# A four-layer graph network on one core: no check between the two steps of layer 3, and one sum and one branch at the end

## The chip, the cores and the metric

The kernel runs on one core of a Trainium2 chip. The metric is the device time of one execution in microseconds (us), as the median of several. A core has five instruction engines that run side by side and wait for one another through semaphores: TensorE (PE, with its weight loads as PEld), VectorE (DVE), ScalarE (ACT), GpSimd (POOL) and SyncE (SP), which here issues most DMAs.

## The reference

A node matrix x of 3327 x 256 goes through four layers, each as x + layer(relu(layernorm(x))), with one adjacency matrix adj of 3327 x 3327 (about 1% of it is not zero, every value is at least 0). Everything is float32.

```python
# layer 0: adj @ (h @ W.T + b)
# layer 1: sim = tanh(adj * adj), of each row the 700 largest entries, times a projected h
vals, idx = jax.lax.top_k(filt, 700)
# layer 2: relu(D^-1/2 (adj + I) D^-1/2 @ (h @ W.T))
# layer 3: two steps
R = S + I;  R = R / R.sum(-1, keepdims=True)            # S is adj
for n in range(2):
    probs = softmax((Xa @ W1.T @ W2.T) @ (Xa @ W3.T).T)
    A = probs, of each row the largest entries until their sum reaches 0.9, renormalised
    Xf = R @ Xf
    Xa = A @ Xa
    Z = Z + Xf @ U1[n].T + Xa @ U2[n].T
out = x + layernorm(X + Z)
```

Two things in it depend on the data. Layer 1 keeps 700 entries of a row, which is all of them unless a row has more than 700 that are not zero. Layer 3 needs, for every row of 3327 probabilities, the threshold at which the kept ones reach 0.9.

## The kernel before

**Tiles.** The 3327 nodes are padded to T = 26 tiles of 128 rows. The products with the adjacency matrix (layers 0 to 2, and `Xf = R @ Xf` in layer 3) take tiles in pairs, m and m + 13, and form the four blocks of a pair from seven products, as Strassen and Winograd do. In layer 3 these are `PropagatedPair` (matmuls L1182), whose operands are "slabs" of 832 KB in three buffers, loaded by SyncE (L1147) and partly corrected by POOL (L1151).

**Attention in layer 3.** For each of the two steps and each tile: eight logits matmuls in four chunks of two PSUM banks (L962), each chunk evicted by ScalarE with exp and a row sum (L983, `exp_of_logits`); then `search_steps`, which looks for the row's threshold. That is a chain of six small ScalarE operations (L1000 to L1005), a ScalarE pass over the 3328 columns (`junk_a`, relu, L1016), a second pass (sign, L1021; for the first tile of a step, which is `alone`, VectorE does it, L1019), and VectorE passes: L1032, four partial passes L1041 with 26 `max` of eight (L1045), some small operations, and L1061, which zeroes what is below the threshold in the tile `e` and sums the rest. TensorE then turns `e` in 128 x 128 blocks (`pt`, L186), ScalarE copies them (`eT`, L189), and TensorE multiplies them with the nodes (L197). The tiles of the second step come in the order 0, 13, 1, 14, and so on; three are in work at a time.

**Guards.** The search starts from an estimate and can fail for a row. `failed(step, st)` compares the kept sums of all 26 tiles with their targets, lets a matmul with ones (`pf`, L1093) add up the rows that failed, and reduces that by threes (L1099) to four levels of counts, of which the last holds the total. `if_failed` then loads the total into a register of every engine (L1406) and branches (`tc.If`, L1407); behind the branch lies a nested tree that leads to each tile, with code that searches it again (`by_least`, and `general` behind a further branch) and recomputes what came from it. The kernel holds one such check between the steps and one after the second step. A third guard, for layer 1: `most1` is the largest count of entries in a row, copied as an integer into `flag`; at the end `at_end()` loads it (L1732), and `tc.If(loaded[0] > TOPK)` (L1735) leads to a second pass over layers 1 to 3, `all_layers(True)`, in which layer 1 searches for the 700th entry. In the data at hand no count is above zero and no row above 700, so each branch passes its code over.

**What sets the order.** On TensorE the order is written out by hand (`tc.manual_schedule(engines=PE_ALONE)`, with `spread`, `merged` and `plan` naming which steps go between which matmuls). A planner places the instructions of the other engines by costs and priorities; `tc.high_priority()` and `tc.issue_after(x)` bend it. Each engine runs its instructions in the planned order. A branch parts the program: nothing is planned across it. So the check between the steps separates the end of step one (the propagation of pair 12, phase one, and the logits of tiles 0 and, in part, 13 of step two) from the rest. Two lines stand behind it: the `memset` of one column of `w`, and `only_exp_and_ln()` (L873), a load of ScalarE's function table.

Of the kernel before, what the change touches and what calls it, by code (L numbers as in the profile page):

```python
# [11 lines left out]
F32 = mybir.dt.float32  # L12
I32 = mybir.dt.int32
# [4 lines left out]
ALU = mybir.AluOpType  # L18
# [6 lines left out]
P = 128  # L25
T = 26
NP = T * P
# [5 lines left out]
TOPK = 700  # L33
# [13 lines left out]
def kernel(  # L47
# [22 lines left out]
    nc = tc.nc  # L70


    const = ctx.enter_context(tc.tile_pool(name="const", bufs=1))
# [798 lines left out]
    def only_exp_and_ln():  # L872
        tc.keep_in_program_order(nc.scalar.preload_act_table_set("natural_log_exp_and_others"))  # L873

    def layer_3(again, h3, kT0, ksum0, left, at_end):
        tag = "b" if again else "a"

        only_exp_and_ln()
        with ExitStack() as lctx:
            big, ep, w3, sm3 = (  # L880
                lctx.enter_context(tc.tile_pool(name=f"{n}{tag}", bufs=b))
                for n, b in (("big", 1), ("ep", 3), ("w3", 2), ("sm3", 4))
            )
            layer_3_in(tag, big, ep, w3, sm3, h3, kT0, ksum0, left, at_end)

    def layer_3_in(tag, big, ep, w3, sm3, h3, kT0, ksum0, left, at_end):

# [9 lines left out]
        w = big.tile([P, 7 * P], F32, name="w")  # L899
# [174 lines left out]
        LEVELS = 3  # L1074
# [262 lines left out]
        spare = []  # L1337
# [64 lines left out]
        def if_failed(step, flags, st, kT, then, scratch, at_last):  # L1402
            def inside(level, i, gen):
                if i * 3**level >= T:
                    return
                n = nc.values_load(flags[level].bitcast(I32)[0:1, i : i + 1])  # L1406
                with tc.If(n > 0):  # L1407
                    if level:
                        with tc.tile_pool(name=f"gen{step}", bufs=1) if not gen else nullcontext(gen) as g:
                            for k in range(3):  # L1410
                                inside(level - 1, 3 * i + k, g)
                        if level == LEVELS:
                            at_last()
                    else:
                        e, den, bad = by_least(step, i, kT, gen, st, scratch)
                        then(i, e, den, f"t{i}")
                        n_bad = nc.values_load(bad)
                        with tc.If(n_bad > 0):
                            then(i, *general(step, i, kT, gen, scratch), f"g{i}")

            inside(LEVELS, 0, None)

        kT1, ksum1 = new_keys(f"1{tag}", big)
# [11 lines left out]
        with tc.manual_schedule(engines=PE_ALONE):  # L1435

            st0, made, dens, props = new_state("0"), {}, {}, []
# [85 lines left out]
            for i in range(EARLY):  # L1523
                plan = {}
# [21 lines left out]
            for m in range(T):  # L1546
                interleaved = m + AHEAD < T and m not in APART
                plan, later = passes_apart(0, finder) if interleaved else (passes(finder), {})
                plan = merged(plan, left_over)
# [63 lines left out]
        def redo_second_steps_first():  # L1613
            run(exp_of_logits(1, 0, kT1, first_e, first_parts, "again"))

        if_failed(0, flags0, st0, kT0, redo_first, lambda name: first_e, redo_second_steps_first)

        nc.vector.memset(w[:, 0:1], 0.0)  # L1620
        only_exp_and_ln()
        with tc.manual_schedule(engines=PE_ALONE):
            st1 = new_state("1")
            run(find(1, 0, st1))
            rows_of_first(H - 2)
            p = props.pop(0)
            propagate_first(T - 2, merged(spread(steps_of_second, 0, 6), {3: [lambda: p.scale(last_exp)], 8: [p.turn], 12: [p.sums]}))
            p = props.pop(0)
            second = find(1, ORDER[1], st1)

            def pass_of_second():
                with tc.issue_after(last_exp[-1].ins):
                    next(second)

            plan = {0: [lambda: p.scale(last_exp)], 3: [p.turn], 8: [p.sums], 15: [lambda: next(second), pass_of_second], 19: [pass_of_second]}
            propagate_first(T - 1, merged(spread(prepare(1, ORDER[2], kT1), 4, 10), plan))
            run(second)
            finder = find(1, ORDER[2], st1)
            fs.append(new_nodes(f"fs{tag}")[:, :, :D])
            for k in range(0, T, H):  # L1640
                for a, b in ((k, k + 6), (k + 6, k + H - 1)):
                    nc.scalar.dma_start(fs[0][:, a:b, :], fs_dram[:, a:b, :])
            rows_of_first(H - 1)

            def propagate_second(m, at):
                acc = new_acc(f"f1_{m}")
                run(propagated_steps(acc, 1, m, fs[0]), at)
                return acc

            rows = Rows(1, vs)  # L1650
            rows.begin(0)
            flags1 = []
            ts = new_ts(1)
            ys, stores = {}, []
            for i, m in enumerate(ORDER):
                ahead = ORDER[i + AHEAD] if i + AHEAD < T else None
                plan, later = passes_apart(1, finder) if ahead else (passes(finder), {})
                if i == 0:
                    p, q = props
                    plan = merged(plan, {2: [p.scale, q.scale], 4: [p.turn], 5: [p.sums, q.turn], 6: [q.sums]})  # L1660
                acc = rows.finish(m, plan)
                if i == 0:
                    nc.sync.dma_start(gs, ln_g.partition_broadcast(P))
                    nc.sync.dma_start(bs, ln_b.partition_broadcast(P))
                ys[m] = attention_of_second_step(m, acc, dens.pop(m), f"{m}")
                plan = spread(prepare(1, ahead, kT1)) if ahead else {}
                if i + 1 < T:
                    plan = merged(plan, {20: [lambda: rows.begin(ORDER[i + 1])]}, later)
                else:
                    plan = {4: [lambda: flags1.extend(failed("1", st1))]}  # L1670
                if i == 1:
                    with tc.issue_after(last_found[-1].ins):
                        for c in CUTS:
                            combine(fs[0], ts, *c)
                p, phase = m % H, m // H
                if p == 0:

                    finish3(m, ys.pop(m), propagate_second(m, plan)[:, :D], f"{m}")()
                else:
                    if not phase:  # L1680
                        pair = PropagatedPair(1, p, fs[0], ts)

                        def stores_of_last():

                            with tc.issue_after(pair.loaded.ins):
                                while stores:
                                    stores.pop(0)()

                        plan = merged(plan, {22: [stores_of_last]})
                    units = H * len(PHASES[phase])  # L1690
                    run(pair.steps(phase), {k * units // T: v for k, v in plan.items()})
                    if not phase:
                        pair.half()
                    else:
                        both = pair.whole()
                        for j, k in ((1, m), (0, p)):
                            if pair.last and not j:
                                pair.ended()
                            stores.append(finish3(k, ys.pop(k), both[:, j, :], f"{k}"))
                finder = find(1, ahead, st1) if ahead else None  # L1700
            for store in stores:
                store()

        def redo_second(m, e, den, name):
            y = attention_of_second_step(m, rows_times(e, vs, w3, f"a1_{name}"), den, name)
            finish3(m, y, propagate_second(m, {})[:, :D], name)()

        at_end()
        spare.append(ep.tile([P, NP], F32, tag="e", name=f"spare{tag}"))
        if_failed(  # L1710
            1, flags1, st1, kT1, redo_second, lambda name: ep.tile([P, NP], F32, tag="e", name=name), lambda: None
        )


    def all_layers(again, at_end):
        with tc.manual_schedule(engines=PE_ALONE):
            lctx, h3, kT0, ksum0, left = layers_0_to_2(again)
            lctx.close()
            if not again:

                nc.vector.tensor_reduce(most, counts, AX.X, ALU.max)
                pm = one_bank("pm")
                nc.tensor.transpose(pm[:1, :P], most, ident)
                nc.vector.tensor_reduce(most1, pm[:1, :P], AX.X, ALU.max)
                nc.vector.tensor_copy(flag, most1)
        layer_3(again, h3, kT0, ksum0, left, at_end)

    most = const.tile([P, 1], F32, name="most")
    most1 = const.tile([1, 1], F32, name="most1")
    flag = const.tile([1, 1], I32, name="flag")  # L1730
    loaded = []
    all_layers(False, lambda: loaded.append(nc.values_load(flag[0:1, 0:1])))  # L1732


    with tc.If(loaded[0] > TOPK):  # L1735
        all_layers(True, lambda: None)


# [44 lines left out]
```

## The time and the profile before

| | us |
|---|---|
| three runs | 2583.54, 2582.86, 2580.24 (median 2582.86) |
| the profiled execution: its time | 2582.32 |
| its span, first to last instruction | 2580.5 |
| layers 0 to 2, until about | 960 |
| layer 3, first step, until the check | 960 to 1796.5 |
| around the check: TensorE busy | 8.7 of 15.0 (1796.5 to 1811.5) |
| second step: TensorE busy | 748.9 of 757.5 (1811.5 to 2569) |
| from the last arithmetic to the end of the span | 11.5 |

TensorE's mean granted clock over the span is 0.994 of full speed. One execution is profiled; its time is the metric, and its span is 1.8 us shorter, because the time also holds what lies ahead of the first and behind the last recorded instruction. Engines' busy times are given as sums over the span. In a timeline, brackets hold how long the engine had been idle before the instruction and which instruction is inferred to have ended that; a "q" behind an engine's name stands for the engine's queue of register, branch and semaphore instructions, which do not count as busy.

### The profile page before, as it was taken

To read this page: it belongs to the slowest core of one execution; us is meant where nothing else is said; L and a number is where in the kernel's file an instruction comes from. 1 tells how busy PE (TensorE), PEld (TensorE's weight loads), DVE (VectorE), ACT (ScalarE), POOL (GpSimd) and SP (SyncE) were. 2 spreads that over 40 slices of the span, in tenths; PEclk is the share of its full clock that TensorE was granted. 3 is DMA by queue.
4 is the path that set the end of the run, shared out by engine and by line. 5 is a ranking of instruction groups with operands and counts; after the bars stand their busy time and mean duration, and the time that the engine had idled before them with its cause. 6 is when DMAs were issued, how large, how long until landed. Compare 5 with 4: busy or idle time off the path is not lost. (4 is left out here: it accounts for less than half of the span.)

```text
span 2580.5 us, 47702 instructions
## 1 busy us (share of the span) xinstructions
PE 2514.0 (97%) x17929; PEld 2255.6 (87%) x17929; DVE 2082.3 (81%) x5538; ACT 1083.7 (42%) x2055; POOL 293.1 (11%) x485
## 2 busy tenths in 40 slices
PE   7999999999999999999999999998999999999997
PEld 7999999999999998878787878787888888888886
DVE  6667788888878778787778787784899899899994
ACT  3110123343111115555656566653555555555551
POOL 2000010000000001000000000000021122212132
PEclk9999999999999999999999999999999999999999
DMA  6677765555788865323232323232433343344342
GB/s 222 191 227 249 220 197 182 166 173 171 250 294 269 280 208 186 107 65 107 69 103 92 107 67 102 61 113 97 159 119 106 112 135 111 112 141 130 106 135 84
DMA packets 181794, 388.47 MB, mean 151 GB/s; under 512 B 19742, under 2 KB 78747, under 8 KB 181531
## 3 DMA queue, kind: packets, MB, share of 16 engines
q1 hardware_dynamic: 153210, 364.31, 43.7%
q10 hardware_dynamic: 28320, 20.80, 2.5%
q8 instruction: 147, 2.41, 0.4%
q14 instruction: 117, 0.95, 0.1%
HBM read 315.44 MB, written 67.89 MB: 149 GB/s over the span
## 5 line engine op out<-in xcount | busy, mean ns | idle before, releaser
L189 ACT COPY eT_a<-pt_a 128x512 f32<-128x512 f32 (+1 forms) x364 | 195.8, 554 | 361.2 <-PE pt_a L186 361.0
L197 PE MATMUL a<-h3a,eT_a 128*128 128x256 f32 x1352 | 325.7, 383 | 0.2 <-ACT eT_a L189 0.2
L197 PE MATMUL a<-vs,eT_a 128*128 128x256 f32 x1352 | 320.3, 381 | 0.2 <-ACT eT_a L189 0.2
L1045 DVE MAX8 cand_a<-w 128x8 f32<-128x128 f32 x1352 | 290.0, 279 | 4.5
L197 PEld LDWEIGHTS a<-h3a,eT_a 128*128 128x128 f32 x1352 | 245.7, 191 | 37.5 <-issue 5.7
L197 PEld LDWEIGHTS a<-vs,eT_a 128*128 128x128 f32 x1352 | 244.7, 190 | 30.2 <-ACT eT_a L189 0.7
L557 PE MATMUL acc_a<-tsa,s_a 128*128 128x128 f32 (+1 forms) x2028 | 269.1, 275 | 0.0
L557 PE MATMUL acc_a<-rhs,a_a 128*128 128x128 f32 (+1 forms) x2028 | 251.4, 277 | 0.1
L557 PE MATMUL acc_a<-tsa,a_a 128*128 128x128 f32 x2028 | 250.3, 275 | 0.9 <-DVE tsa L351 0.9
L557 PEld LDWEIGHTS acc_a<-tsa,s_a 128*128 128x128 f32 x2028 | 248.2, 192 | 0.3
L557 PEld LDWEIGHTS acc_a<-rhs,a_a 128*128 128x128 f32 x2028 | 239.3, 192 | 2.2 <-ACT rhs L436 0.4
L557 PEld LDWEIGHTS acc_a<-tsa,a_a 128*128 128x128 f32 x2028 | 239.1, 192 | 2.1 <-DVE tsa L351 1.3
L1041 DVE SCALAR_TENSOR_TENSOR w<-e_a,t_a 128x896 f32<-128x896 f32 x208 | 225.0, 1082 | 4.4
L983 ACT ACTIVATE e_a<-pl_a 128x1024 f32<-128x1024 f32 x208 | 177.8, 860 | 108.6 <-PE pl_a L962 108.6
L186 PE MATMUL pt_a<-ident,e_a 128*128 128x128 f32 x1352 | 199.9, 274 | 6.9 <-DVE e_a L1061 6.6
L186 PEld LDWEIGHTS pt_a<-ident,e_a 128*128 128x128 f32 x1352 | 165.9, 141 | 36.5 <-DVE e_a L1061 7.2
L1151 POOL TENSOR_TENSOR slab3a<-slab3a,ident 128x128 f32<-128x128 f32 x100 | 104.2, 1043 | 814.5 <-DMA slab3a<-in_adj_t_dram 379.1
L1061 DVE SCALAR_TENSOR_TENSOR e_a<-e_a,all_least 128x3328 f32<-128x3328 f32 x52 | 194.4, 3739 | 1.8
L1032 DVE SCALAR_TENSOR_TENSOR w<-e_a,t_a 128x3328 uint8<-128x3328 f32 x52 | 191.7, 3686 | 4.0
L395 ACT ACTIVATE xT_a<-pt_a 128x512 f32<-128x512 f32 x52 | 30.8, 593 | 356.6 <-PE pt_a L391 300.5
L1182 PEld LDWEIGHTS f0a<-tsa,slab3a 128*128 128x128 f32 x1352 | 160.2, 192 | 16.9 <-issue 13.9
L688 ACT ACTIVATE a_a<-a_a 128x640 f32<-128x640 f32 (+1 forms) x156 | 101.4, 665 | 174.2 <-DVE a_a L687 152.9
(246 smaller groups left out, 4224.2 us busy)
## 6 DMA issues: line engine op xcount, KB each, us to landing
slab3a<-s_dram SPq DMA_DIRECT2D x100, 832.0 KB, 4.6
a_a<-in_adj_t_dram SPq DMA_DIRECT2D x312, 256.0 KB, 4.1
slab3a<-in_adj_t_dram SPq DMA_DIRECT2D x79, 832.0 KB, 4.6
a_a<-in_adj_t_dram SPq DMA_DIRECT2D x156, 320.0 KB, 3.8
s_dram<-s_a SPq DMA_DIRECT2D x78, 256.0 KB, 4.9
s_dram<-s_a SPq DMA_DIRECT2D x39, 320.0 KB, 5.2
x_dram<-x_a ACTq DMA_DIRECT2D x39, 256.0 KB, 3.5
s_dram<-a_a SPq DMA_DIRECT2D x26, 256.0 KB, 5.2
```

The source lines that it names most:

```text
L186: nc.tensor.transpose(pt[:, j, :], e[:, k * P : (k + 1) * P], ident)
L189: last_turned.append(nc.scalar.copy(eT[:, : len(blocks), :], pt[:, : len(blocks), :]))
L197: nc.tensor.matmul(acc[:, :width], ready[g][:, j, :], rhs[:, k, :], start=(k == 0), stop=(k == T - 1))
L557: nc.tensor.matmul(self.acc[:, g, at : at + wide], quads[n][:, k - CUTS[c][0], :], t, start=(k == 0 and n in (1, 4)), stop=(k == H - 1 and ...
L688: nc.scalar.activation(a, a, AF.Tanh)
L983: last_exp.append(nc.scalar.activation(dst, src, AF.Exp, accum_out=parts[:, c : c + 1]))
L1032: nc.vector.scalar_tensor_tensor(junk, e, t, e, ALU.is_lt, ALU.mult, accum_out=got)
L1041: nc.vector.scalar_tensor_tensor(w[:, : (b - a) * P], eg, t, eg, ALU.is_lt, ALU.mult, accum_out=below[:, g : g + 1])
L1045: nc.vector.max(cand[:, 8 * k : 8 * k + 8], w[:, (k - a) * P : (k - a + 1) * P])
L1061: nc.vector.scalar_tensor_tensor(e, e, least, e, ALU.is_ge, ALU.mult, accum_out=st["kept"][:, m : m + 1])
L1151: nc.gpsimd.tensor_tensor(x[:, p, :], x[:, p, :], ident, ALU.add)
L1182: nc.tensor.matmul(self.accs[bank][:, c * P : (c + 1) * P], a, self.right(n, k), start=start, stop=last.get(bank) == (n, k), skip_group_ch ...
```

## The change

The check after step one, the check after step two, the `memset` and the table load behind the first are now in the program only in the second pass (`if again`). In the first pass the last tile's step `last_flags` forms one number, `redo`: 1 if `most1` is over 700, plus the total of failures of the first step, plus that of the second. After the store of the results one register is loaded from it, and one branch leads to the second pass, which holds the checks of single tiles and the search of layer 1. The integer copy `flag` is gone. A failed tile, which was redone alone before, would now cost a whole second pass.

```diff
-        if_failed(0, flags0, st0, kT0, redo_first, lambda name: first_e, redo_second_steps_first)
-
-
-
-        nc.vector.memset(w[:, 0:1], 0.0)
-        only_exp_and_ln()
+        if again:
+            if_failed(0, flags0, st0, kT0, redo_first, lambda name: first_e, redo_second_steps_first)
+            nc.vector.memset(w[:, 0:1], 0.0)
+            only_exp_and_ln()
+
         with tc.manual_schedule(engines=PE_ALONE):
             st1 = new_state("1")
...
-                    plan = {4: [lambda: flags1.extend(failed("1", st1))]}
+                    def last_flags():
+                        flags1.extend(failed("1", st1))
+                        if not again:
+                            nc.vector.scalar_tensor_tensor(
+                                redo, most1, float(TOPK), flags0[LEVELS], ALU.is_gt, ALU.add
+                            )
+                            nc.vector.tensor_tensor(redo, redo, flags1[LEVELS], ALU.add)
+
+                    plan = {4: [last_flags]}
...
-        at_end()
-        spare.append(ep.tile([P, NP], F32, tag="e", name=f"spare{tag}"))
-        if_failed(
-            1, flags1, st1, kT1, redo_second, lambda name: ep.tile([P, NP], F32, tag="e", name=name), lambda: None
-        )
-
-
-    def all_layers(again, at_end):
+        if again:
+            spare.append(ep.tile([P, NP], F32, tag="e", name=f"spare{tag}"))
+            if_failed(
+                1, flags1, st1, kT1, redo_second, lambda name: ep.tile([P, NP], F32, tag="e", name=name), lambda: None
+            )
+
+
+    def all_layers(again):
...
-                nc.vector.tensor_copy(flag, most1)
-        layer_3(again, h3, kT0, ksum0, left, at_end)
+        layer_3(again, h3, kT0, ksum0, left)
...
-    flag = const.tile([1, 1], I32, name="flag")
-    loaded = []
-    all_layers(False, lambda: loaded.append(nc.values_load(flag[0:1, 0:1])))
-
-
-    with tc.If(loaded[0] > TOPK):
-        all_layers(True, lambda: None)
+    redo = const.tile([1, 1], F32, name="redo")
+    all_layers(False)
+    n_redo = nc.values_load(redo.bitcast(I32)[0:1, 0:1])
+
+
+    with tc.If(n_redo > 0):
+        all_layers(True)
```

More of the change, by code (lines that the diff above doesn't have):

```diff
@@ L873, in only_exp_and_ln, with layer_3 @@
         tc.keep_in_program_order(nc.scalar.preload_act_table_set("natural_log_exp_and_others"))
-    def layer_3(again, h3, kT0, ksum0, left, at_end):
+    def layer_3(again, h3, kT0, ksum0, left):
         tag = "b" if again else "a"
@@ L883, in layer_3, with layer_3_in @@
             )
-            layer_3_in(tag, big, ep, w3, sm3, h3, kT0, ksum0, left, at_end)
-    def layer_3_in(tag, big, ep, w3, sm3, h3, kT0, ksum0, left, at_end):
+            layer_3_in(again, tag, big, ep, w3, sm3, h3, kT0, ksum0, left)
+    def layer_3_in(again, tag, big, ep, w3, sm3, h3, kT0, ksum0, left):
         def new_ts(step):
```

## The prediction

> **What bounds the kernel now.** I read the page's busy shares first, then the table of stretches around the check between the two steps of layer 3, the timelines of TensorE and ScalarE there, the instructions of the check's own lines, and last the end of the run. The page's first section:
>
> ```profile
> PE 2514.0 (97%) x17929; PEld 2255.6 (87%) x17929; DVE 2082.3 (81%) x5538; ACT 1083.7 (42%) x2055; POOL 293.1 (11%) x485
> ```
>
> TensorE is the bound. After the check it hardly stops again (the waits of PE from 1796 us on hold, beside the check, only 2.5, 1.1, 0.3 and 0.2 us), so what it loses at the check arrives at the end unless another engine takes it. The timeline of TensorE there (start, length, what, and in brackets the idle time before it and who ended that):
>
> ```profile
> 1795.86 0.71 PE L1182 MATMUL f0a<-h3a,slab3a 128*128 128x128 f32 x4
> 1799.73 0.46 PE L1182 MATMUL f0a<-h3a,slab3a 128*128 128x128 f32 x2 [3.15 <-ACT mean_a L1001]
> 1803.31 4.14 PE L962 MATMUL pl_a<-kT_1a,qT 64*128 64x512 f32 x8 [3.12 <-DVEq L1407]
> 1807.38 2.94 PE L1182 MATMUL f0a<-h3a,slab3a 128*128 128x128 f32 x24
> 1810.26 1.35 PE L962 MATMUL pl_a<-kT_1a,qT 64*128 64x512 f32 x8
> ```
>
> Two holes, 3.15 and 3.12 us: the first is TensorE's own branch, the second its wait for VectorE's (ACT in the first bracket is inferred; ScalarE was done). The logits at 1803.31 then take 4.14 us, where the eight that began at 1790.68 took 1.99. The table of stretches says why: the column after POOL is the granted clock.
>
> ```profile
> 1800.20:1803.30 3.10, 0.00 (x0) 0.02 (x1) 0.00 (x0) 0.60 (x3) 0.00 (x0) 0.52 0.09 30
> 1803.30:1807.40 4.10, 4.09 (x9) 2.25 (x9) 4.01 (x6) 3.88 (x3) 0.56 (x2) 0.53 0.25 73
> 1807.40:1811.60 4.20, 4.20 (x34) 3.49 (x33) 3.94 (x7) 1.85 (x6) 0.00 (x0) 1.00 0.16 24
> ```
>
> The lines of the branches (duration in ns min/median/max, first and last start):
>
> ```profile
> L1407 PEldq COMPARE_BRANCH  x2: 3342/3620/3897, 1795.3 to 2562.9; - x2
> L1407 DVEq COMPARE_BRANCH  x2: 72/72/72, 1798.8 to 2569.0; - x2
> L1407 DVEq EVENT_SEMAPHORE  x4: 21/21/21, 1803.1 to 2572.7; - x4
> L1732 SPq TENSOR_LOAD <-flag x1: 273/273/273, 2573.5 to 2573.5; - x1
> L1735 SPq EVENT_SEMAPHORE  x9: 17/17/17, 2576.8 to 2579.1; - x9
> ```
>
> VectorE's branch at 1798.8 takes 0.07 us by its record, but its next instruction stands at 1803.1. So a branch over skipped code costs an engine 3 to 5 us, on TensorE inside the branch's record, on the others as silence after it. At the end the last arithmetic (DVE L1293) stops at 2569.1 us and the span at 2580.5: 11.4 us of stores landing, two branches in turn (L1407, L1735) and a closing barrier.
>
> [...]
>
> **The change part by part.** The instruction order of the changed program, engine by engine, is that of the old one without the check, but for the moves named here.
>
> *The check between the steps goes.* On the old clock: TensorE is done at 1796.57, and without the branch issues its next two matmuls at once (0.25 us), then the eight logits of tile 13, chunks 0 and 1 (1.99 at full clock), then 24 propagation matmuls (2.94). That is 1801.8; chunk 2 ends at 1802.8. Chunk 3 needs the PSUM bank of chunk 1, and here ScalarE decides:
>
> ```profile
> 1797.03 0.20 ACT L983 ACTIVATION_READ_ACCUMULATOR e_a<-pl_a 128x1 f32 x1
> 1799.11 0.21 ACT L1000 ACTIVATE parts_a<-parts_a 128x5 f32<-128x5 f32 x1 [1.88 <-ACTq L1407]
> 1803.52 3.07 ACT L1016 ACTIVATE junk_a<-e_a,t_a 128x3328 uint8<-128x3328 f32 x1 [2.66 <-POOLq L1407]
> 1806.59 1.00 ACT L983 ACTIVATE e_a<-pl_a 128x1024 f32<-128x1024 f32 x1
> ```
>
> Without its 1.88 us it goes from 1797.2 through the small chain L1000 to L1005 (1.75 us, from 1799.11 to 1800.86) to 1799.0. In the new order the eviction of chunk 0 stands before the pass L1016, not behind it: 1.0, to 1800.0. Then the pass, 3.07, to 1803.1; then the eviction of chunk 1 with its accumulator, 1.2, to 1804.3. So TensorE waits 1.5 us at chunk 3 and is through at about 1804.7, where the old one was at 1811.54. **Gain 6.8 us**: 6.3 of holes and 2.15 of low clock (4.14 less 1.99), less 1.5 of a new wait for ScalarE.
>
> Does anyone take it back? VectorE's search of tile 0 started at 1803.86 (L1019). It needs t, now ready at 1799.0: 4.75 us earlier, less some 0.3 for the new place of ScalarE's pass, whose sum L1027 reads. These rows say what that is worth:
>
> ```profile
> 1828.35 3.68 DVE L1061 SCALAR_TENSOR_TENSOR e_a<-e_a,all_least 128x3328 f32<-128x3328 f32 x1
> 1836.54 1.04 PE L186 MATMUL pt_a<-ident,e_a 128*128 128x128 f32 x8
> ```
>
> TensorE needs e of tile 0 at 1836.54, 4.5 us after VectorE is done; new 1829.7 against 1827.6, so 2.1 us of cover remain. From tile 13 on, VectorE's search hangs on ScalarE's passes, which are placed behind TensorE's own transposes, and moves with TensorE. SyncE: the two loads of z (L1278) move from behind the check to before the store of z of tile 25 and before slab 5's load. The first waits for nothing late. The second waits for that store (issued 1787.85, stores of z land in 1.9 us, so 1789.8), and the queue stood at 1790.15 then anyway for a slab. Slab 5 goes out at 1796.6 as before, when its buffer comes free, lands 4.6 us later and is needed at about 1809.8. POOL's additions and the later slabs follow TensorE's releases. Cost nothing.
>
> *The table load and the memset* (1.28 us at 1784.87 on ScalarE, which then waits for matmuls until 1786.99; 0.06 us on VectorE): gain nothing. *Two additions of failures*, about 0.16 us each like the reductions L1099: the first falls into VectorE's wait until 1784.45, the second into its 3.59 us before 2561.76. *The copy of the count into `flag`* (0.14 us at 956.3) stood before a wait for ScalarE: nothing. *At layer 3's start* one of ScalarE's key evictions now stands behind a copy (0.26) and a weight load's issue (0.48). It ended at 969.83, and VectorE, busy till 970.93, reads it then: hidden, 0.3 us of loss at the worst, since TensorE waits for VectorE at tile 0 there (2.41 us).
>
> *At the end one branch goes.* SyncE ends last: store, load of the register, branch, nine waits, and all that again. From its second load at 2573.5 to the first wait after that branch at 2576.8 is 3.3 us, and one set of nine waits 0.6 (the first set, 0.07 apart): **gain 3.9 us**. The second set took 2.3 us, with a silence of 1.7 in it[...]. It may go too (5.6), or the remaining branch may take as much longer (2.2). Stores set no later limit: the last was issued at 2569.1 and lands after 4.6 in the median, 2573.7, about when the one set of waits ends (2573.5).
>
> Sum: 6.8 + 3.9 = 10.7 us. The profiled execution took 2582.32 (span 2580.5 and 1.8 around it), so 2571.6. The median of the runs shown is 0.54 higher: **2572.1 us**. Bounds of the middle: 4.5, if VectorE's earlier start were all that counts, and 8.4, if ScalarE were never waited for. Bounds of the end: 2.2 and 5.6. Together 6.7 to 14.0.
>
> **The rivals.** *Full gain*, as above, 80 in 100. *ScalarE or VectorE becomes the bound of the second step's start*: the order around chunk 3 and the first tiles is tight (2.1 us), and more waits such as the 1.11 before pt_f could grow. For it: ScalarE is busy without a break from 1797 on. Against: no wait of TensorE for e in the whole second step. Middle 3, end 3: 2576.9, 12 in 100. *Only the end gains*: the lead is absorbed by a later wait with a fixed place, as the slab load that TensorE waits 2.5 us for near the end; that one hangs on TensorE's own progress, which speaks against. 2579, within 0.2%, 5 in 100. *Slower*: slab 5's load on SyncE is held by the z load now ahead of it, until the store of z it reads has landed. As worked out, that store lands at 1789.8 and the queue is free long before 1796.6. The slab is needed at about 1809.8 and takes 4.6 to land and about 1 for POOL's addition (L1151), so the store would have to land after 1804 before TensorE lost anything, after 1815 before the whole 10.7 were lost, and after 1820 to make the kernel slower by 0.2%, 30 us beyond the times that stores of z take here: about 2588, 2 in 100. *It does not do what it says*: a failed tile in this data would bring the second pass over three layers, thousands of us. The old branches L1407 and L1735 were both passed over in the trace, so the same sums are zero: 1 in 100.
>
> **How the numbers follow.** 0.2% (5.2 us) is about what a measurement of this kernel can tell from no change. Faster by more: 80 + 12 = 92; within: 5; slower: 3. The range reaches from the upper bound of both parts (14.0: 2568.9), less about half of the 3.3 us that the runs shown lie apart, to the second case and as much beyond it: 2567 to 2578.5. That leaves out the last three cases, 8 in 100, and what the bounds of the first missed.
>
> **What would show it.** In the changed profile: no record of L1406 between 1783 and 1804; TensorE's granted clock 1.00 there; one hole of about 1.5 us at the last logits of tile 13, before an ACT release; VectorE's L1061 of tile 0 ending about 2 us before TensorE's transposes; one TENSOR_LOAD on SyncE, and some 7.5 us from the last arithmetic to the end of the span. Wrong would be: a wait of TensorE for VectorE's e of tile 0, a slab awaited at the start of the second phase, or the span after the last arithmetic still at 11 us.

## The result, and the profile after

The changed kernel takes **2564.89 us** in the median of six runs (2563.0 to 2567.4), the kernel before 2580.77 (2577.72 to 2583.54): ratio 0.9938, 95% interval 0.9925 to 0.9951. A second measurement, below, gave 0.9943 (0.9930 to 0.9956). So it is faster by about 15.7 us, and 2564.89 lies 2.1 us below the lower end of the predicted range. The profiled execution took 2566.14, with a span of 2564.2.

The page's busy shares (TensorE busy 5 us less in a span 16.3 us shorter, so most of the difference is idle time):

```profile
PE 2509.0 (98%) x17929; PEld 2251.3 (88%) x17929; DVE 2081.6 (81%) x5538; ACT 1082.3 (42%) x2054; POOL 295.8 (12%) x485
```

TensorE's timeline at the place where the check was:

```profile
1792.62 1.99 PE L962 MATMUL pl_a<-kT_1a,qT 64*128 64x512 f32 x8
1794.54 2.94 PE L1182 MATMUL f0a<-h3a,slab3a 128*128 128x128 f32 x24
1797.42 1.13 PE L962 MATMUL pl_a<-kT_1a,qT 64*128 64x512 f32 x4
1799.82 0.49 PE L962 MATMUL pl_a<-kT_1a,qT 64*128 64x128 f32 x4 [1.28 <-ACT e_a L983]
```

Both holes of 3.1 us are gone, the eight logits take 1.99 us instead of 4.14, and one hole of 1.28 us stands before the last logits, released by ScalarE. The table of stretches has the granted clock at 1.00 in both stretches (the column after POOL's sum is clock, then the share of the DMA engines and GB/s):

```profile
1792.30:1797.40 5.10, 4.97 (x34) 3.45 (x33) 4.25 (x9) 4.91 (x14) 0.65 (x3) 1.00 0.53 167
1797.40:1799.80 2.40, 1.15 (x5) 0.30 (x4) 2.14 (x7) 2.40 (x5) 0.00 (x0) 1.00 0.48 136
```

ScalarE's timeline shows why the hole is there. The pass L1016 stands between the evictions of tile 13's first and second chunk, and the last logits want the bank that the second one empties.

```profile
1794.62 1.00 ACT L983 ACTIVATE e_a<-pl_a 128x1024 f32<-128x1024 f32 x1
...
1795.62 3.06 ACT L1016 ACTIVATE junk_a<-e_a,t_a 128x3328 uint8<-128x3328 f32 x1
...
1798.67 1.01 ACT L983 ACTIVATE e_a<-pl_a 128x1024 f32<-128x1024 f32 x1
```

VectorE's last pass over tile 0 in step two, from its own timeline, ends at 1823.19 (with the read of the accumulator behind it):

```profile
1819.51 3.69 DVE L1061 SCALAR_TENSOR_TENSOR e_a<-e_a,all_least 128x3328 f32<-128x3328 f32 x1
```

TensorE's timeline has the transposes that need it at 1825.24, so the cover has shrunk from 4.50 to 2.05 us:

```profile
1825.24 1.04 PE L186 MATMUL pt_a<-ident,e_a 128*128 128x128 f32 x8
```

At the end, the lines of the one branch on SyncE (durations in ns, then the first and last start):

```profile
L1741 SPq EVENT_SEMAPHORE  x9: 17/17/17, 2562.3 to 2562.9; - x9
L1741 SPq COMPARE_BRANCH  x1: 50/50/50, 2559.5 to 2559.5; - x1
```

One set of nine waits, over in 0.6 us. From the last arithmetic (2558.47) to the end of the span it is 5.8 us, where it was 11.4.

To see where the time went, the execution is cut at four points of TensorE's and VectorE's work that every kernel here has: the last attention matmul of step one (L197, ahead of the check), the first of step two (behind it), TensorE's last matmul, and the last VectorE result (L1293). Between the third and the fourth lie 4.5 us everywhere. These are my sums from the traces, in us, one profiled execution each:

| kernel | start to check | across the check | step two | last result to end |
|---|---|---|---|---|
| before | 1780.7 | 57.1 | 726.8 | 11.4 |
| before, second profile | 1774.9 | 57.1 | 730.8 | 11.3 |
| changed | 1776.4 | 50.1 | 727.5 | 5.8 |
| changed, second profile | 1773.3 | 50.1 | 727.5 | 5.7 |

Across the check the gain is 7.0 us, at the end 5.6. Of the rest of the difference between the two first profiles, 4.3 us arose before the place of the check, where both programs do the same work; in step two the changed kernel was 0.7 us slower.

### The profile page after: what moved, and what is told of

It reads as the page before. It is cut to its first block, busy times and chain, and to the rows that moved or that the text cites. A ratio compares the mean times of both kernels' runs of the same rounds, so it can differ in the third digit from the quotient of the medians.

```text
span 2564.2 us, 47615 instructions
## 1 busy us (share of the span) xinstructions
PE 2509.0 (98%) x17929; PEld 2251.3 (88%) x17929; DVE 2081.6 (81%) x5538; ACT 1082.3 (42%) x2054; POOL 295.8 (12%) x485
## 5 line engine op out<-in xcount | busy, mean ns | idle before, releaser
L197 PE MATMUL a<-h3a,eT_a 128*128 128x256 f32 x1352 | 324.4, 382 | 0.2 <-ACT eT_a L189 0.2
L197 PE MATMUL a<-vs,eT_a 128*128 128x256 f32 x1352 | 320.3, 381 | 0.2 <-ACT eT_a L189 0.2
L197 PEld LDWEIGHTS a<-h3a,eT_a 128*128 128x128 f32 x1352 | 245.1, 190 | 37.2 <-issue 5.7
L197 PEld LDWEIGHTS a<-vs,eT_a 128*128 128x128 f32 x1352 | 244.7, 190 | 30.3 <-ACT eT_a L189 0.7
L1032 DVE SCALAR_TENSOR_TENSOR w<-e_a,t_a 128x3328 uint8<-128x3328 f32 x52 | 192.1, 3694 | 4.0
L1182 PEld LDWEIGHTS f0a<-tsa,slab3a 128*128 128x128 f32 x1352 | 160.2, 192 | 17.0 <-issue 13.9
```

The lines of the kernel that those rows point to most:

```text
L197: nc.tensor.matmul(acc[:, :width], ready[g][:, j, :], rhs[:, k, :], start=(k == 0), stop=(k == T - 1))
L1032: nc.vector.scalar_tensor_tensor(junk, e, t, e, ALU.is_lt, ALU.mult, accum_out=got)
L1182: nc.tensor.matmul(self.accs[bank][:, c * P : (c + 1) * P], a, self.right(n, k), start=start, stop=last.get(bank) == (n, k), skip_group_ch ...
```

## The experiments

### The two kernels again, and each half of the change alone

The theory (A): the gain is made at the two places, and the lead ahead of the check is chance of single executions. The rival (B): the lead belongs to the changed program. Two kernels take one half of the change each.

```diff
# mid_only: before, without the check between the steps
-        if_failed(0, flags0, ...)
-        nc.vector.memset(w[:, 0:1], 0.0)
-        only_exp_and_ln()
+        if again:
+            if_failed(0, flags0, ...)
+            nc.vector.memset(w[:, 0:1], 0.0)
+            only_exp_and_ln()
...
# end_only: the changed kernel, with those lines unconditional again
```

> The kernel before, unchanged, to see how far single executions lie apart and where. Theory A (the 4.3 us that the changed kernel's profile is ahead by before it reaches the place of the check are chance of one execution: where TensorE's clock falls to half for 3.4 us): 2580.8 us, single executions 2 to 3 us to either side, the low-clock stretches of this profile elsewhere than at 660 and 1022 us. Theory B (the lead belongs to the changed program): low-clock stretches again at 660 and 1022, the logits in front of the check again at 1790.5 within 1 us.

Measured: 2580.39 us (13 runs, 2574.64 to 2584.59; 30 runs of the shared comparison 2580.17, 2577.15 to 2584.54). Single executions of one program do lie up to 10 us apart. Ahead of the check the first profile has four stretches of 3.4 us in which TensorE's granted clock is half (at 25, 660, 1022 and 1261 us, by the trace's clock record). This one has two, at 27 and 1016 us, and one more at 2535, and it reached the check 5.9 us earlier. B had asked for 1 us and the same places, so it fails here. In each such stretch TensorE is busy all the time, so each costs it an estimated 1.7 us, half its length. Two more of them make 3.4 of the 5.9 us.

> The changed kernel, unchanged. Theory A: 2565 us and a gain of 12 to 16; in its profile the first logits of tile 13 (the eight L962 that began at 1786.4) lie between 1786 and 1791, by how many low-clock stretches fall ahead of them. Theory B: again at 1786.4 within 1 us.

Measured: 2564.67 us, ratio 0.9943 (0.9930 to 0.9956), and the check's place reached 3.2 us earlier than in its first profile, so that these logits began at 1783.2, ahead of what either theory gave. Their place moves by microseconds within one program. That is against B's 1 us, and A's span was too narrow. The changed kernel's first profile has two half-clock stretches ahead of this place, at 25 and 1257 us, where that of before has four. So 3.4 of the 4.3 us by which it leads there are, by the same estimate, stretches that fell otherwise.

> The kernel before without the check between the steps (and its memset and table load), with both branches at the end. In all engines the order up to the end is that of the changed kernel, but for a key eviction and a load at the start of layer 3, which stand as before. Sum by parts (A): 7.1 us at the place of the check, less up to 0.7 that a late slab takes back, nothing at the end: 2574 us, ratio 0.9974. If the lead of 4.3 us comes with the shorter program (B): 2570. If nothing reached the end (C): 2580.8. At the end the chain from the last arithmetic stays at 11.4 us, or 9.7 if the 1.7 us of silence within the second set of waits depends on where the code lies.

Measured: 2569.99 us, ratio 0.9961 (0.9948 to 0.9974): 10.2 us less than before, more than A's 7 and with an interval from 6.7 to 13.4. In the profile: 50.1 us across the check, so 7.0 gained there, and 10.1 from the last result to the end, though both branches are still there. SyncE's waits behind the second branch stand within 0.6 us, without the silence that they had before:

```profile
L1734 SPq EVENT_SEMAPHORE  x9: 17/17/17, 2567.2 to 2567.8; - x9
```

So 8.2 of the 10.2 are at the two places, and the silence hangs on where the code lies. The time alone does not part the theories: 2569.99 is B's figure of 2570, and A's, with the silence gone, is 2572.3, which the interval (2566.8 to 2573.5) holds as well. A's figure without that, 2574, is missed.

> The changed kernel with the check between the steps kept as before (with its memset and table load): one sum and one branch at the end alone. Up to the check the order is that of the changed kernel, with the moved key eviction. Sum by parts (A): 3.9 us for a branch and a set of waits as predicted plus 1.7 for the silence: 5.6, so 2575.2 us; 2576.9 if the silence stays. If the lead of 4.3 us hangs on the moved key eviction and load at the start of layer 3 (B): 2571.

Measured: 2575.03 us, ratio 0.9977 (0.9970 to 0.9985): 5.1 us less. The profile has 56.6 across the check and 5.5 from the last result to the end. A holds at the end with 5.6 (5.8 in this profile) and nothing more, and its time of 2575.2 was met. The moved key eviction at the start of layer 3 is in this kernel, and B's 2571 for it was missed. The two halves, 10.2 and 5.1, make 15.3 of the 15.5 to 15.9 us that the whole change gains.

### What the price of the check is: the branch, or the code that it jumps over

```diff
# bare_branch: the changed kernel, in the first pass
+        else:
+            n_first = nc.values_load(flags0[LEVELS].bitcast(I32)[0:1, 0:1])
+            with tc.If(n_first > 0):
+                nc.vector.memset(w[:, 0:1], 0.0)
# skip_pe_40, _200, _2000: in that If also
+                fill = one_bank("fill")
+                for _ in range(200):
+                    nc.tensor.transpose(fill[:1, :P], most, ident)
# skip_dve_400: instead 400 of the memsets
```

> The changed kernel with one register load and one branch back between the steps, over a single memset instead of the tree of redo code, and no table load. It asks what of the check's price is the code that is jumped over. From the last attention matmul of step one to the first of step two (L197) the kernels with the check took 56.5 to 57.1 us, those without it 50.0. If a branch as such costs it (every engine stops, nothing is planned across[...]): 56 to 57, TensorE idle 3 to 6 us at that place, a low-clock stretch of 6.8, time 2572. If the distance costs it: 50.5 to 52, idle about 1, no low clock, time 2566. In between: 53 to 55 with one low-clock stretch of 3.4.

Measured: 2565.18 us, ratio 0.9941 (0.9927 to 0.9954), and 51.1 across the place, with no low clock there. All five engines load a register and branch, and it costs about 1 us. TensorE's own branch is hidden behind queued matmuls; 0.4 us of the cost is a longer wait for ScalarE before the last logits (1.68 instead of 1.28), and 0.4 a wait for a slab. My prediction's sentence that a branch costs an engine 3 to 5 us was wrong as it stood. The branch's own record on TensorE (ns):

```profile
L1622 PEldq COMPARE_BRANCH  x1: 236/236/236, 1792.1 to 1792.1; - x1
```

> The same with 40 transposes to jump over. [...]the branch costs 0.24 us as over one memset; if every jump over more than a few costs a fetch, 3 us or more as with 200. It tells between a short reach and a long one; no theory of the case hangs on it.

Measured: 0.24 us again, and 50.3 across. That is less than with the bare branch, and here VectorE and SyncE branch only after TensorE, not ahead of it: the 1 us hangs on the order around the branch as well.

> The changed kernel with a load and a branch between the steps over one memset and 200 transposes on TensorE, which never run. The bare branch over one memset cost TensorE 0.24 us inside the branch and 1 us from L197 to L197 (51.1 instead of 50.0). If the price of the check is each engine's own distance to the branch's target: TensorE's branch takes 3 to 4 us, as in the check (3.90), the other engines' branches stay short; L197 to L197 some 54 to 56, with at least one low-clock stretch of 3.4 us. If the price came from elsewhere in the check (the nested tree, the table load, several engines stopping together): as the bare branch, 51.

Measured: 50.3 across the place, not 54 to 56. The branch took longer, but began while TensorE still had matmuls queued, and was hidden:

```profile
L1622 PEldq COMPARE_BRANCH  x1: 958/958/958, 1789.8 to 1789.8; - x1
```

> The same with 400 memsets on VectorE to jump over, and nothing on TensorE. Own distance: VectorE is silent 3 to 5 us from its branch (which stood at 1786.1 with the bare branch, 6 us before it has work), TensorE's branch stays at 0.24 us, and L197 to L197 stays at 51: the fetch of an engine that is early is hidden. That would say that in the check it is TensorE's own fetch that makes the first hole, and that VectorE's makes the second only because its branch stood as late as TensorE's. If a far jump of one engine held the others: 53 or more.

Measured: VectorE's next record stands 2.94 us behind its branch, TensorE's branch took 0.24, and it is 51.1 across, as with the bare branch. So this early engine's jump was hidden.

> As with 200 transposes to jump over on TensorE, with 2000 (the tree behind the check holds 3999 matmuls). 200 cost TensorE 0.96 us in the branch and nothing from L197 to L197 (50.3), where I had expected 3 to 4. If a longer jump has to fetch its target from memory[...]: 3 to 4 us in the branch, a hole of TensorE of about 3, one low-clock stretch at most, 53 to 55 from L197 to L197. If TensorE's own distance hardly matters and the check's 3.5 to 3.9 come from all five engines fetching at once: about 1 us again, 50.3 to 51.

Measured: 52.6 across. The branch on TensorE took as long as that of the check (3.4 to 3.9 in the four profiles that have it):

```profile
L1622 PEldq COMPARE_BRANCH  x1: 3460/3460/3460, 1787.1 to 1787.1; - x1
```

and TensorE's timeline has a hole and slow logits behind it:

```profile
1790.77 0.46 PE L1182 MATMUL f0a<-h3a,slab3a 128*128 128x128 f32 x2 [2.42 <-PEq L1622]
1791.16 2.99 PE L962 MATMUL pl_a<-kT_1a,qT 64*128 64x512 f32 x8
```

So TensorE's own far jump makes a hole like the first one of the check, without the other engines' help. It costs 2.5 us here: roughly 2.4 of hole and 1.6 of slow matmuls (granted clock 0.50 from 1792.0 to 1795.4), less the wait of 1.28 us for ScalarE, which is gone. The other 4.5 us of the check's 7.0 were not taken apart by a run. The trace of before puts the second hole down to VectorE, whose branch in the check stood at 1798.85, after TensorE's, and which was silent for 4.3 us until 1803.14, just before the logits start; outside the check itself no kernel here has VectorE jump far at so late a place. The four kernels with code to jump over ran once each, in 2566.5 to 2567.9 us, so only their profiles are compared. TensorE's branch took 0.24 us over no transpose (bare_branch) and over 40, 0.96 over 200 and 3.46 over 2000, and VectorE was silent for 2.94 us behind its jump over 400 memsets. What sets these steps no run shows. In the trace of before, eleven instruction transfers, of 8,192 or 16,384 bytes, start around the check, from 1794.1 to 1804.4 us; in the first profile of the changed kernel none starts between 1789.9 and 1801.0.

### The end

```diff
# shift_3: before, at the start of the program
+    shift = const.tile([1, 8], F32, name="shift")
+    for k in range(3):
+        nc.sync.dma_start(shift[0:1, k : k + 1], ln_g[k : k + 1].partition_broadcast(1))
```

> The kernel before with three tiny loads more on SyncE at the start (some of layer 0's small operations trade places with it), which moves all of SyncE's later code by three instructions. If the silence of 1.75 us within the second set of nine waits is the fetch of a page of instructions, it moves from behind the fifth wait to behind the second. If it is a wait for a store to land, it stays in front of the sixth, that of the store's semaphore.

Measured: the silence moved. In the kernel before, SyncE's waits of the last branch that stand ahead of it are five (the count after the operation):

```profile
L1735 SPq EVENT_SEMAPHORE  x5: 17/17/17, 2576.8 to 2577.1; - x5
```

With three instructions more at the start they are two:

```profile
L1738 SPq EVENT_SEMAPHORE  x2: 17/17/17, 2580.3 to 2580.4; - x2
```

and the third follows 2.2 us after the second. So it belongs to a place in SyncE's code, and is no wait for a store. The trace of before has two instruction transfers of 8,192 bytes inside the silence, at 2577.38 and 2577.42. In this run too there are two such transfers in the silence, at 2580.59 and 2580.87. Its time, 2586.12, is a single one; layer 0's matmuls ran some 4.6 us later than in the kernel before.

> The changed kernel without the load and the branch at the end; the second pass is left out of the program altogether, so that nothing is redone if a search fails. From the last arithmetic to the end of the span 5.7 us become 2.4 (less 0.5 for the load and 2.8 from branch to next wait), or 3.5 to 4 if the last store's landing then decides: 2562 us, ratio to before 0.9928. If the size of the program or its place in memory speeds the first layers up (the theory left from the first four runs for some 2 us ahead of the check), then layer 3's first matmul (L1182) lies well ahead of the 950.8 to 954.3 of the kernels without the check, at 949 or earlier, and the time is 2560 or less.

Measured: 2562.05 us, ratio 0.9923 (0.9910 to 0.9937), and 3.05 us from the last result to the end: the load and the branch that remain cost 2.7 us. SyncE then waits until 2558.93 for the last store, issued at 2557.21, so it is the store that limits. Layer 3's first L1182 stands at 952.9, within the other kernels' 950.8 to 954.3. With the second pass gone from the program nothing was clearly faster ahead of the check (1774.3 us to its place), so the program's size as the source of the lead falls.

### The new wait for ScalarE

```diff
# evict_first: the changed kernel
-            run(find(1, 0, st1))
+            first_find = find(1, 0, st1)
+            next(first_find)
+
+            def pass_of_first():
+                with tc.issue_after(last_exp[-1].ins):
+                    next(first_find)
+                run(first_find)
...
-            propagate_first(T - 2, merged(spread(steps_of_second, 0, 6), {3: ...
+            propagate_first(T - 2, merged(spread(steps_of_second, 0, 6), {0: [pass_of_first], 3: ...
```

> The changed kernel with ScalarE's pass L1016 of tile 0 put behind the eviction of tile 13's second chunk: the 1.28 us hole of TensorE before the last logits should close. If that hole is what is left of the gain there: 50.0 us from L197 to L197 become 48.7, unless VectorE, which gets the sum of the pass 1.1 us later, ends tile 0's L1061 too late (cover 2.05 us, less 1.28 and 1.1: short by 0.3): 49.1. Time 2564, not to be told from the changed kernel. If VectorE's search is held up more, its lateness is the new bound: 50.5 to 51 and a wait of TensorE for e.

Measured: 49.15 across the check's place, so 0.94 us better than the changed kernel, with the hole of 1.28 us gone and 0.10 us of cover left for tile 0. A hole of 0.36 us, again for ScalarE, opens behind the last logits:

```profile
1797.68 1.35 PE L962 MATMUL pl_a<-kT_1a,qT 64*128 64x512 f32 x8
1798.96 1.16 PE L1182 MATMUL f0a<-h3a,slab3a 128*128 128x128 f32 x8
1800.49 0.44 PE L146 MATMUL pt_f<-ident,xf_0a 128*128 128x128 f32 x2 [0.36 <-ACT xf_0a L1256]
```

The time, 2565.93, cannot be told from 2564.7. The hole was most of what was left to gain at this place, and VectorE stands right behind it.

## Why the prediction was right or wrong

**The check between the steps: right.** 6.8 us forecast, 7.0 measured, with 50.09 us across the place in each of the four profiles that have no branch there and the planned order. (The prediction's shorter sum, 6.3 and 2.15 less 1.5, makes 6.95 and not 6.8.) The pieces hold too: the hole before the last logits 1.28 (forecast 1.5), clock 1.00, cover at tile 0 2.05 (forecast 2.1), no wait for VectorE's e, no late slab at the start of step two. The reason given for the holes was too broad. A branch over one instruction (0.24 us on TensorE) did not bring such holes, a far one on TensorE (3.46 us) brought one of 2.42 us, like the first. The prediction's 3 to 5 us for a branch also leave out the shortest in the same trace, ScalarE's 2.4 and SyncE's 2.7 at the end, and the longest, SyncE's 5.6 in the check. That the low clock would go with the holes was an estimate of mine.

**The end: the mechanism right, one term too small.** 3.9 us forecast, 5.6 measured. This is the step that failed: the silence of 1.7 us, which I had kept for the remaining branch. It belongs to a place in SyncE's code, and the remaining set of nine waits does not lie across it. I had named that case (5.6) as a bound. By mid_only, which has both branches and no silence (10.1 us), the parts are 1.2 for the silence and 4.3 for the branch and its waits; only their sum is firm.

**The base: too high.** I stood the sum on the median of three runs, 2582.86; 30 runs gave 2580.17. That is 2.7 us of the 7.2 by which the forecast of 2572.1 missed. The end is 1.7, the check 0.2, and some 2.6 are left, for which the next two paragraphs have no sure owner.

**What TensorE meets after the check: left out.** I costed the second step at nothing beyond its start. In step two, the three profiles with the check (before twice, end_only) average 729.4 us, and five without any branch there (mid_only, the changed kernel twice, no_last_branch, evict_first: 727.5 to 728.5) 728.0. The difference, 1.4 us, is not clean: before itself had 726.8 once and 730.8 once. The two executions with 730.7 and 730.8 wait 0.8 and 1.0 us for POOL's correction of a slab, then 3.8 and 3.9 us for the last slab, where the first profile of before waits 2.5, and a half-clock stretch follows that second wait. Neither comes from the check alone: skip_pe_200 and skip_pe_2000, which do not hold it, wait for POOL too (0.8 and 1.0), and three of the five without a branch have a stretch at the last slab. POOL's timeline in the second profile of before:

```profile
1976.99 2.77 POOL L1151 TENSOR_TENSOR slab3a<-slab3a,ident 128x128 f32<-128x128 f32 x1 [8.21 <-DMA slab3a<-in_adj_t_dram]
```

and VectorE's there, whose pass L1032 the correction outlasts by 0.3 us:

```profile
1975.76 3.69 DVE L1032 SCALAR_TENSOR_TENSOR w<-e_a,t_a 128x3328 uint8<-128x3328 f32 x1
```

The same correction in the changed kernel's second profile came before that pass:

```profile
1966.62 0.46 POOL L1151 TENSOR_TENSOR slab3a<-slab3a,ident 128x128 f32<-128x128 f32 x1 [6.49 <-DMA slab3a<-in_adj_t_dram]
```

So the correction took 2.77 us beside the pass and 0.46 ahead of it. In the first profile of before, 30 of the 100 corrections began during an L1032. Each ended 0.31 to 0.32 us behind it, after 1.12 to 3.73 us; the other 70 took 0.46 us in the median. In the first profile of the changed kernel 31 of 32 did the same, and one that began 0.03 us behind the start of the pass took 0.46. Why the slab lands later in those executions was not tried.

**What stays open.** 7.0 and 5.6 make 12.6, and the 1.4 of step two, if they belong to the change, make 14.0; measured were 15.9 and 15.5. The intervals of both ratios (12.6 to 19.4 and 11.4 to 18.1) reach these sums, so nothing more need be there. But the executions without the far check (ten, shift_3 with its late start not counted on either side) reached its place after 1772.5 to 1778.1 us, 1775.5 on average, and the three with it after 1774.9 to 1780.7, 1778.1 on average. The ranges overlap, and neither the moved key eviction nor the program's size accounts for it. Half-clock stretches account for 1.4 of the 2.6: with half of TensorE's busy time in them taken off, the averages are 1772.4 with the far check and 1771.4 without, in ranges of 1771.5 to 1773.9 and 1769.1 to 1773.3. These stretches fall differently from one execution to the next, so over many runs they need not favour either kernel. Whether a real lead of 1 us or so is left, the runs do not tell.

**The range** failed because its lower end took the base as sure: the upper bounds of both parts (14.0) off 2580.2 would have reached 2566.2, and the 1.9 us between the prediction's own bound (2568.9) and its range (2567) would have brought it to 2564.3, past 2564.9. Of the rivals none came true.

## What to carry to other kernels

A check that is never taken can be nearly free: 0.2 to 1.1 us across its place where TensorE jumps over at most 200 transposes, 7 us in the check with its some 4000 matmuls of redo code. Part of its price is the far jump of the engine that is the bound (2.5 us in skip_pe_2000). The rest goes, by the trace of before but by no run of its own, to engines that jump late, and a far jump early on an engine with spare time was hidden (skip_dve_400). When a gain is costed from one execution, stand it on as many runs as there are, and put every silence that has no owner into the range on both sides.

## What the runs showed of the hardware that was not expected

- TensorE's half-clock stretches last 3.4 us while it has work, or twice that (6.8 in the first profile of before, from 1800.3), and begin on a fixed grid within an execution, in another place in the next. In the first profile of before they begin at 660.3, 1022.1, 1261.0 and 1800.3 us, which lie 106, 70 and 158 times 3.413 us apart, the length of a short stretch in the trace's clock record. The same wait, such as that of 1.9 to 2.4 us for tile 0 near 1018, is followed by the low clock in some executions and not in others.
- How the wait lies on that grid goes far to tell which. With the fourteen profiles cut into windows of 3.413 us on each one's grid, from about 45 us on, all 41 windows in which TensorE was idle for 1.92 us or more are followed by half clock. Of seven with 1.79 to 1.91, four are; of those with less, a single one, which itself lay behind a half-clock window (shift_3, at 2538). So the low clock follows holes shorter than the two of 3.1 us in the check, too: one of 2.01 us in the second profile of before, at 1014.4, one of 2.42 us in skip_pe_2000.
- Straight-line code stopped as well: for 1.7 us in the first profile of before and 2.2 us in shift_3, at one place of SyncE's code shortly behind a far jump, which three instructions more at the start of the program moved by three instructions.
